# Nodes' places worked out in 128 rows behind the second table, and a written order with late sums in the message stage of a graph layer

## The chip, the core and the metric

The kernel runs on one core of a Trainium2 chip. The metric is the device time of one execution in microseconds (us). TensorE (PE), VectorE (DVE), ScalarE (ACT), GpSimd (POOL) and SyncE (SP) each run their own instructions in order, and wait for each other with semaphores. SP does no arithmetic here: it starts transfers between memory and the core's SBUF. POOL starts the indirect transfers, which gather rows of a table by a list of numbers.

## What is computed

One graph layer on 12,500 nodes with 96 features and 412,500 edges, all in float32. The edges are sorted by their target node `dst`.

```python
def _mlp(h, W, b, gamma, beta):
    h = relu(h @ W + b)
    mu, var = mean(h, axis=0), mean((h - mu)**2, axis=0)
    return gamma * (h - mu) * rsqrt(var + EPS) + beta

node_feat = _mlp(x, W_node, ...)
edge_feat = _mlp(edge_attr, W_edge, ...)          # 4 -> 96 features
message   = _mlp(concat([x[src], x[dst], edge_feat]), W_msg, ...)
agg       = segment_sum(message, dst)             # sum of the messages into each node
out       = layernorm(x + agg + node_feat)
```

## The kernel before

The product with `W_msg` is split into its three blocks of 96 rows. `x` times the first block gives the table `p_tab`, `x` times the second gives `q_tab`; both are stored in memory by `table()` (L137), which makes 14 columns of 128 nodes at a time, in 7 pieces, through the SBUF tile `trow`. A message then is relu(p_tab[src] + q_tab[dst] + edge part).

Edges go in tiles of 128, groups of 4 tiles (512 edges, 806 groups) and blocks of 4 groups (202 blocks). The stages, in the order of the program:

1. `p_tab` (L156), loads of small weights, and a check of the graph (L172 to L190).
2. Nodes' places (L192 to L201): for each edge, its target minus the first target of its group, as float32, written to memory as `rel_d`. The 413,696 numbers are laid out in 101 rows of 4096, and done in four parts of 1024 columns. Loads (`lin`, `first`) are issued by SP, the stores of `rel_d` by ACT. The tiles have two buffers each.
3. `fast()` (L286). Inside a block in which SP and POOL keep the written order (L309), it makes `q_tab`, then the node features (`nodes()`, L203, which end in 13 stores `y0_d`), then the mean and variance of the edge features (`edge_norm()`, L235: 26 loads of 8 blocks, for each block three matmuls on different rows of the array, one ReLU over all three on ACT, three `bn_stats` on DVE).
   While these run, POOL gathers ahead. `blocks()` (L298) gathers `p_tab` rows for the first 26 blocks (104 groups, 416 indirect transfers) into the tile `stage`, which has two buffers, and SP stores each block to `spill` in memory. Each `next(store)` puts one block's 16 gathers into POOL's order and its one store into SP's order at that point. So a store of `spill` stands in SP's queue between the stores and loads of the stage that is running, and the gathers of block b+2 can begin only when the store of block b has landed. After the 26 blocks, POOL fills a ring of 30 groups (L325).
4. The message stage (L327 to L439). The 176 late blocks take their `p_tab` rows from the ring, as POOL delivers them; the 26 early blocks take them back from `spill` (`fetch`, L410). The written order of blocks spreads the early ones among the late ones. For each block `load()` brings edge attributes, `rel_d` and four windows of `q_tab`, and `prepare()` makes the left operand `left` (relu of the edge part, and rows that mark the place: L371 matmuls into four PSUM banks, L373 on ACT, L374 on DVE). For each group `message()` makes z (4 matmuls, L380), adds the gathered rows (L386) and takes the ReLU (L387); `reduce()` multiplies the group's messages with themselves and with the marks of the targets (4 matmuls, L395) and adds the result to `agg` (L398) and to `gram` (L399), which gives mean and variance of the messages. `reduce` of a group stands one group behind its `message`. Here no order is fixed by hand: a scheduler orders each engine.
   POOL's part in it: after a group, the gather of the group 30 ahead is asked for (L436).
5. The final stage (L607): `agg` is scaled, turned to rows, added to `y0_d`, normalised and stored.

SBUF is handed out by pools: a pool that closes gives its space to the next, and the first write into the new tile waits until the last use of the old one is done. The tiles `lin` and `rlin` of stage 2 and `trow` of the second table lie in such shared space.

Of the kernel before, what the change touches and what calls it, by code (L numbers as in the profile page):

```python
# [11 lines left out]
F32 = mybir.dt.float32  # L12
I32 = mybir.dt.int32
# [9 lines left out]
P = 128  # L23
# [12 lines left out]
RW = 8 * GE  # L36
# [18 lines left out]
RING = 30  # L55
CL, CE = 2, 2
# [15 lines left out]
def gnn(ctx, tc, t):  # L72
# [7 lines left out]
    rel_d = dram.tile([1, EP], F32, name="rel_d")  # L80
# [56 lines left out]
    def table(out, w, work, ps, queues):  # L137

        rows = out.rearrange("(p b) f -> p b f", b=NB)
        for c in range(0, NB, CH):  # L140
            r = work.tile([P, CH, C], F32, name="trow", bufs=3)
            for j, i in enumerate(range(0, CH, NBK)):
                n = min(NBK, CH - i)
                pt = ps.tile([P, NBK, C], F32, name="pt", bufs=4)
                for g in range(n):
                    k = COL[c + i + g]
                    nc.tensor.matmul(pt[:, g, :], xp[:, k:k + P], w, start=True, stop=True)  # L147
                if j % 2:
                    nc.scalar.activation(r[:, i:i + n, :], pt[:, :n, :], AF.Copy)  # L149
                else:  # L150
                    nc.vector.tensor_copy(r[:, i:i + n, :], pt[:, :n, :])
            queues[c // CH % len(queues)].dma_start(rows[:, c:c + CH, :], r)
            yield

    with tc.tile_pool(name="win_w", bufs=1) as work, tc.tile_pool(name="win_ps", bufs=2, space=PSUM) as ps:
        for _ in table(p_tab, w_msg[:, 0, :], work, ps, (nc.sync, nc.scalar)):  # L156
            pass
# [34 lines left out]
    with tc.tile_pool(name="lin", bufs=2) as work:  # L192
        shape = "o (p g e) -> (o p) g e"
        for i in range(0, RW // GE, 2):
            lin = work.tile([EP // RW, 2, GE], I32, name="lin")
            nc.sync.dma_start(lin, t["dlin"].rearrange(shape, g=RW // GE, e=GE)[:, i:i + 2, :])
            first = work.tile([EP // RW, 2], I32, name="first")
            nc.sync.dma_start(first, t["base"].rearrange("o (p g) -> (o p) g", g=RW // GE)[:, i:i + 2])
            rlin = work.tile([EP // RW, 2, GE], F32, name="rlin")
            nc.vector.tensor_tensor(rlin, lin, first.unsqueeze(2).to_broadcast([EP // RW, 2, GE]), op=OP.subtract)  # L200
            nc.scalar.dma_start(rel_d.rearrange(shape, g=RW // GE, e=GE)[:, i:i + 2, :], rlin)  # L201
# [33 lines left out]
    def edge_norm():  # L235

        with tc.tile_pool(name="es", bufs=2) as work, tc.tile_pool(name="es1", bufs=1) as one, \
                tc.tile_pool(name="es_ps", bufs=2, space=PSUM) as ps:
            stats = one.tile([P, NS, NBL, 6], F32, name="estats")
            for b in range(NBL):  # L240
                if b % J == 0:
                    yield
                    ea = work.tile([P, J, GE], F32, name="ea")
                    n = min(J, NBL - b)
                    for i in range(NS):
                        nc.sync.dma_start(ea[Q * i:Q * i + 2 * EK, :n, :],
                                          t["ea"][EK * i:EK * (i + 2), b:b + n, :])
                pr = ps.tile([P, NS, GE], F32, name="pr")
                for i in range(NS):
                    nc.tensor.matmul(pr[:, i, :], wide[Q * i:Q * i + 2 * EK, :],  # L250
                                     ea[Q * i:Q * i + 2 * EK, b % J, :], start=True, stop=True)
                r = work.tile([P, NS, GE], F32, name="r")
                nc.scalar.activation(r, pr, AF.Relu)  # L253
                for i in range(NS):
                    nc.vector.bn_stats(stats[:, i, b, :], r[:, i, :])  # L255
# [30 lines left out]
    def fast(ring):  # L286
# [22 lines left out]
        with tc.manual_schedule(engines={ET.SP, ET.Pool}):  # L309
            with tc.tile_pool(name="tab_w", bufs=1) as work, tc.tile_pool(name="tab_ps", bufs=2, space=PSUM) as ps:  # L310
                for i, _ in enumerate(table(q_tab, w_msg[:, 1, :], work, ps, (nc.sync,))):
                    if i in (3, 6):
                        next(store)
            next(store)
            next(store)
            for i, _ in enumerate(nodes()):
                if i in (5, 12):
                    next(store)
            xpool.close()
            for i, _ in enumerate(edge_norm()):  # L320
                if i > 1 and i % 5:
                    next(store, None)
            for _ in store:
                pass
            got = {g: ahead_of(g) for g in range(SPILL, SPILL + RING)}  # L325

        with tc.tile_pool(name="fix", bufs=1) as fix, tc.tile_pool(name="msg", bufs=2) as work, \  # L327
# [3 lines left out]
            rhs = fix.tile([P, 2, BG, C], F32, name="rhs")  # L331
            nc.vector.tensor_copy(rhs[:C], w_e[:, None, None, :].to_broadcast([C, 2, BG, C]))
            for i in range(2):
                for k in range(BG):
                    nc.sync.dma_start(rhs[KR - 1:KR, i, k, :], bias)
# [3 lines left out]
            hb = [fix.tile([P, GT, P], F32, name=f"h{i}") for i in range(4)]  # L339
# [3 lines left out]
            eas = {}  # L343

            def load(s, b):

                n = min(BG, NG - b * BG)
                first = SPILL // BG
                c, o = ((b - first) // CL * CL + first, CL) if b >= first else (b // CE * CE, CE)
                if c not in eas:  # L350
# [8 lines left out]
                    base[:, b * BG:(b + 1) * BG], engines=[ET.DVE, ET.SP], min_val=0, max_val=N - 1,  # L359
                    skip_runtime_bounds_check_because="they are nodes' numbers")  # L360
                for i in range(n):
                    nc.sync.dma_start(rhs[C:C + WN, s % 2, i, :], q_tab[bass.ds(val[i], WN), :])
                return ea, val

            def prepare(s, b, ea):

                n = min(BG, NG - b * BG)
                x = left[s % 2]
                pr = ps.tile([C + WN, BG, GE], F32, name="pr", bufs=1)
                for i in range(n):  # L370
                    nc.tensor.matmul(pr[:, i, :], we[Q * i:Q * i + EK + 1, :],  # L371
                                     ea[Q * i:Q * i + EK + 1, :], start=True, stop=True)
                nc.scalar.activation(x[:C, :n, :], pr[:C, :n, :], AF.Relu)  # L373
                nc.vector.tensor_scalar(x[C:C + WN, :n, :], pr[C:, :n, :], 0.0, None, op0=OP.is_equal)  # L374

            def message(s, g, h, pg):
                n = min(GT, NT - g * GT)
                z = ps.tile([P, GT, C], F32, name="z")
                for i in range(n):
                    nc.tensor.matmul(z[:, i, :], left[s % 2][:KR, g % BG, i * P:(i + 1) * P],  # L380
                                     rhs[:KR, s % 2, g % BG, :], start=True, stop=True)
# [7 lines left out]
            def reduce(g, h, val):  # L389

                n = min(GT, NT - g * GT)
                pa = ps.tile([C + 1, P], F32, name="pa")
# [4 lines left out]
                to = agg[:, bass.ds(val, WN)]  # L397
# [4 lines left out]
            early, late = list(range(SPILL // BG)), list(range(SPILL // BG, NBL))  # L402
            order = []
            for i, b in enumerate(late):
                order.append(b)
                while early and (SPILL // BG - len(early)) * len(late) < i * (SPILL // BG):
                    order.append(early.pop(0))
            order += early

            def fetch(b):  # L410
                if b * BG < SPILL:
                    back = work.tile([P, BG, GT, C], F32, name="pb")
                    nc.sync.dma_start(back, spill[b].rearrange("p g (a c) -> p g a c", a=GT))
                    for i in range(BG):
                        got[b * BG + i] = back[:, i, :, :]

            ea, val = load(0, order[0])
            prepare(0, order[0], ea)
            fetch(order[0])
            last, n, ahead = None, 0, SPILL + RING  # L420
            for s, b in enumerate(order):
                more = s + 1 < len(order)
                if more:
                    ea, then = load(s + 1, order[s + 1])
                    fetch(order[s + 1])
                for g in range(b * BG, min((b + 1) * BG, NG)):
                    if g % BG == 1 and more:
                        prepare(s + 1, order[s + 1], ea)
                    h = hb[n % len(hb)]
                    n += 1  # L430
                    message(s, g, h, got.pop(g))
                    if last:
                        reduce(*last)
                    last = g, h, val[g % BG]
                    if g >= SPILL and ahead < NG:
                        got[ahead] = ahead_of(ahead)  # L436
                        ahead += 1
                val = then
            reduce(*last)  # L439
# [235 lines left out]
```

## Time and profile before

| what | value |
|---|---|
| median of 10 runs | 4306.22 us (4305.18 to 4308.59) |
| profiled execution: its own time, its span | 4305.96 us, 4304.2 us |
| PE busy | 3377.8 us (78%), 16,561 matmuls |
| DVE busy | 1812.4 us (42%) |
| ACT busy | 1132.6 us (26%) |
| POOL busy | 3054.0 us (71%), 3,231 instructions |
| moved by DMA | 271.03 MB, mean 63 GB/s |

The own time of the profiled execution is 1.76 us above its span and 0.26 us below the median. Busy times leave out register and branch instructions and the issuing of plain transfers; for POOL's gathers, the time on the engine is counted, and the gap to the next one is not. A matmul in float32 shows as two records. "PEclk" is the clock that TensorE was granted, as a share of the full one.

### The profile page before, as it was taken

To read this page: it belongs to the slowest core of one execution; us is meant where nothing else is said; L and a number is where in the kernel's file an instruction comes from. 1 tells how busy PE (TensorE), PEld (TensorE's weight loads), DVE (VectorE), ACT (ScalarE), POOL (GpSimd) and SP (SyncE) were. 2 spreads that over 40 slices of the span, in tenths; PEclk is the share of its full clock that TensorE was granted. 3 is DMA by queue.
4 is the path that set the end of the run, shared out by engine and by line. 5 is a ranking of instruction groups with operands and counts; after the bars stand their busy time and mean duration, and the time that the engine had idled before them with its cause. 6 is when DMAs were issued, how large, how long until landed. Compare 5 with 4: busy or idle time off the path is not lost. (4 is left out here: it accounts for less than half of the span.)

```text
span 4304.2 us, 52840 instructions
## 1 busy us (share of the span) xinstructions
PE 3377.8 (78%) x16561; PEld 2490.5 (58%) x16561; DVE 1812.4 (42%) x4227; ACT 1132.6 (26%) x1304; POOL 3054.0 (71%) x3231
## 2 busy tenths in 40 slices
PE   4089998778778887887787787777878888878787
PEld 4063222566666666666666666666666666656666
DVE  1057999533333333333333333333333333333334
ACT  0035776222122222222222222222222222212221
POOL 3067777777777777777777777777777777777772
PEclk9975555877777776778768777777776777777775
DMA  4045554222222222222222222222222222222223
GB/s 147 30 135 122 115 107 99 72 54 53 48 51 53 53 52 46 53 52 54 53 45 53 53 54 53 46 53 53 54 53 45 53 53 53 53 44 54 45 45 106
DMA packets 154490, 271.03 MB, mean 63 GB/s; under 512 B 83723, under 2 KB 84107, under 8 KB 153198
## 3 DMA queue, kind: packets, MB, share of 16 engines
q0 software_dynamic: 103136, 158.62, 17.8%
q1 hardware_dynamic: 47572, 96.59, 7.8%
q10 hardware_dynamic: 3496, 12.36, 0.9%
q8 instruction: 136, 2.23, 0.2%
q14 instruction: 150, 1.23, 0.1%
HBM read 225.97 MB, written 41.37 MB: 62 GB/s over the span
## 5 line engine op out<-in xcount | busy, mean ns | idle before, releaser
L290 POOL DMA_INDIRECT pg<-p_tab,src x2807 | 2655.1, 946 | 855.6 <-issue 765.9
L380 PEld LDWEIGHTS z<-rhs,left 128*128 128x128 f32 x6446 | 1111.6, 253 | 732.3 <-DVE hs L386 427.1
L395 PE MATMUL pa<-h 128*97 128x128 f32 x6446 | 1185.0, 343 | 365.7 <-ACT h L387 356.1
L380 PE MATMUL z<-rhs,left 128*128 128x96 f32 x6446 | 1240.5, 343 | 283.4 <-DVE hs L386 277.3
L395 PEld LDWEIGHTS pa<-h 128*97 128x97 f32 x6446 | 1011.4, 216 | 429.0 <-ACT h L387 419.7
L386 DVE TENSOR_TENSOR hs<-z,pg 128x384 f32<-128x384 f32 x702 | 391.0, 557 | 1935.9 <-DMA pg<-p_tab,src 1779.7
L387 ACT ACTIVATE h<-hs 128x384 f32<-128x384 f32 x806 | 420.9, 522 | 2581.6 <-DVE hs L386 1736.5
L290 POOL DMA_INDIRECT stage<-p_tab,src x416 | 398.0, 957 | 326.1 <-DMA spill<-stage 141.2
L371 PE MATMUL pr<-ea,we 6*127 6x512 f32 x1404 | 507.7, 870 | 40.0 <-DVE left L374 30.5
L374 DVE TENSOR_SCALAR left<-pr 31x2048 f32<-31x2048 f32 x202 | 462.9, 2291 | 19.2 <-ACT left L373 12.9
L373 ACT ACTIVATE left<-pr 96x2048 f32<-96x2048 f32 x202 | 375.0, 1857 | 111.8 <-PE pr L371 98.6
L250 PE MATMUL pr<-ea,wide 10*128 10x512 f32 x1212 | 396.1, 1096 | 9.3 <-DMA ea<-in_ea 9.3
L255 DVE BATCH_NORM_STATS2 estats<-r 128x6 f32<-128x512 f32 x606 | 369.5, 679 | 34.2 <-ACT r L253 30.3
L253 ACT ACTIVATE r<-pr 128x1536 f32<-128x1536 f32 x202 | 292.9, 1450 | 156.9 <-PE pr L250 156.9
L250 PEld LDWEIGHTS pr<-ea,wide 10*128 10x128 f32 x1212 | 113.2, 307 | 290.9 <-ACT r L253 267.1
L382 DVE TENSOR_TENSOR h<-rel,iota 128x124 f32<-128x124 f32 x806 | 207.6, 278 | 1.7 <-issue 0.4
L399 DVE TENSOR_TENSOR gram<-pa,gram 97x97 f32<-97x97 f32 x806 | 201.2, 250 | 6.6 <-DVE agg L398 6.5
L398 DVE TENSOR_TENSOR agg<-pa,agg 97x31 f32 x806 | 147.5, 183 | 130.5 <-PE pa L395 128.1
L147 PE MATMUL pt<-w_msg,xp 96*128 96x96 f32 x392 | 85.7, 423 | 138.9 <-ACT trow L149 131.4
L371 PEld LDWEIGHTS pr<-ea,we 6*127 6x127 f32 x1404 | 127.9, 237 | 104.4 <-DVE left L374 52.4
L147 PEld LDWEIGHTS pt<-w_msg,xp 96*128 96x128 f32 x392 | 84.1, 332 | 140.2 <-ACT trow L149 132.2
L386 DVE TENSOR_TENSOR hs<-z,pb 128x384 f32<-128x384 f32 x104 | 57.5, 553 | 84.6 <-ACT left L373 41.9
(97 smaller groups left out, 528.0 us busy)
## 6 DMA issues: line engine op xcount, KB each, us to landing
pg<-p_tab,src POOLq DMA_INDIRECT x2807
spill<-stage SPq DMA_DIRECT2D x26, 768.0 KB
pb<-spill SPq DMA_DIRECT2D x26, 768.0 KB
rhs<-q_tab SPq DMA_DIRECT2D x806, 11.6 KB
ea<-in_ea SPq DMA_DIRECT2D x75, 160.0 KB
ea<-in_ea SPq DMA_DIRECT2D x352, 20.0 KB
stage<-p_tab,src POOLq DMA_INDIRECT x416
q_tab<-trow SPq DMA_DIRECT2D x7, 672.0 KB
```

The lines of the kernel that those rows point to most:

```text
L250: nc.tensor.matmul(pr[:, i, :], wide[Q * i:Q * i + 2 * EK, :], ea[Q * i:Q * i + 2 * EK, b % J, :], start=True, stop=True)
L253: nc.scalar.activation(r, pr, AF.Relu)
L255: nc.vector.bn_stats(stats[:, i, b, :], r[:, i, :])
L290: nc.gpsimd.indirect_dma_start(out=pg[:, i, :], out_offset=None, in_=p_tab[:, :], in_offset=bass.IndirectOffsetOnAxis(ap=src[:, k:k + 1], ...
L371: nc.tensor.matmul(pr[:, i, :], we[Q * i:Q * i + EK + 1, :], ea[Q * i:Q * i + EK + 1, :], start=True, stop=True)
L373: nc.scalar.activation(x[:C, :n, :], pr[:C, :n, :], AF.Relu)
L374: nc.vector.tensor_scalar(x[C:C + WN, :n, :], pr[C:, :n, :], 0.0, None, op0=OP.is_equal)
L380: nc.tensor.matmul(z[:, i, :], left[s % 2][:KR, g % BG, i * P:(i + 1) * P], rhs[:KR, s % 2, g % BG, :], start=True, stop=True)
L382: nc.vector.tensor_tensor(h[:, :, C + 1:C + 1 + WN], rel[:, g, :].unsqueeze(2).to_broadcast([P, GT, WN]), iota[:, None, :].to_broadcast([P ...
L386: nc.vector.tensor_add(hs[:, :n, :], z[:, :n, :], pg[:, :n, :])
L387: nc.scalar.activation(h[:, :n, :C], hs[:, :n, :], AF.Relu)
L395: nc.tensor.matmul(pa[:, :C + 1 + WN], h[:r, i, :C + 1], h[:r, i, :C + 1 + WN], start=i == 0, stop=i == n - 1)
```

## The change

Four edits, and the loop that carries them.

- **Places.** The step moves out of stage 2 into a function `places()`, called behind the second table. The numbers are padded to 128 rows of 7 groups, done in parts of 2, 2, 2 and 1 groups. All transfers are on SP, and the store of a part is issued behind the load of the next.
- **Tables and stores.** The second table gets 8 PSUM buffers. The places of `next(store)` change: three within the second table, one behind `places()`, two within `nodes()` (behind the third and the ninth `y0_d` store), then one at 19 of the 26 loads of `edge_norm()` (73 in 100), the rest behind.
- **Edge statistics.** Matmuls are put in pairs into 4 PSUM tiles of two banks (before: three into 2 tiles of three), with one ReLU for each pair.
- **Message stage.** PE, DVE and ACT keep the written order too. z of group k+1 is asked for ahead of the additions of group k; the products of group k-1 follow; their sums are added at group k+4 (`SKEW = 5` behind k). Four groups' products share one PSUM tile. `prepare` is cut into two halves of two groups, at the third and fourth group of the block before. `left` is unchanged; the right operand `rhs` has 3 buffers (before 2), `h` has 6 (before 4), and `load` runs two blocks ahead (before one).

The core of the diff:

```diff
+    def places():
+        with tc.tile_pool(name="lin", bufs=2) as work, tc.tile_pool(name="lin1", bufs=1) as one:
+            first = one.tile([P, RW], I32, name="first")
+            nc.sync.dma_start(first, t["first"])
+            rows = rel_d.rearrange("o (p g e) -> (o p) g e", g=RW, e=GE)
+            parts = [slice(i, min(i + 2, RW)) for i in range(0, RW, 2)]
+            lins = []
+            for i in range(len(parts) + 1):
+                if i < len(parts):
+                    n = parts[i].stop - parts[i].start
+                    lins.append(work.tile([P, n, GE], I32, name="lin"))
+                    nc.sync.dma_start(lins[i], t["dlin"][:, parts[i], :])
+                    rlin = work.tile([P, n, GE], F32, name="rlin")
+                    nc.vector.tensor_tensor(rlin, lins[i], first[:, parts[i]]..., op=OP.subtract)
+                    lins[i] = rlin
+                if i:
+                    nc.sync.dma_start(rows[:, parts[i - 1], :], lins[i - 1])
...
-                    if i in (3, 6):
+                    if i in (1, 4, 6):
                         next(store)
-            next(store)
+            places()
             next(store)
             for i, _ in enumerate(nodes()):
-                if i in (5, 12):
+                if i in (2, 8):
                     next(store)
             xpool.close()
+            n = 0
             for i, _ in enumerate(edge_norm()):
-                if i > 1 and i % 5:
+                if 73 * i >= 100 * n:
                     next(store, None)
+                    n += 1
...
-                pr = ps.tile([P, NS, GE], F32, name="pr")
                 for i in range(NS):
-                    nc.tensor.matmul(pr[:, i, :], wide[...], ea[...], start=True, stop=True)
-                r = work.tile([P, NS, GE], F32, name="r")
-                nc.scalar.activation(r, pr, AF.Relu)
+                    k = NS * b + i
+                    if k % 2 == 0:
+                        pr = ps.tile([P, 2, GE], F32, name="pr")
+                    nc.tensor.matmul(pr[:, k % 2, :], wide[...], ea[...], start=True, stop=True)
+                    if k % 2:
+                        r = work.tile([P, 2, GE], F32, name="r", bufs=4)
+                        nc.scalar.activation(r, pr, AF.Relu)
...
+            with tc.manual_schedule(engines={ET.SP, ET.Pool, ET.PE, ET.DVE, ET.Activation}):
+                load(0)
+                fetch(0)
+                load(1)
+                edges(0)
+                prepare(0, 0)
+                prepare(0, BG // 2)
+                linear(0)
+                for k in range(n + SKEW):
+                    s, g = steps[min(k, n - 1)]
+                    if k < n and g % BG == 0:
+                        if s + 2 < len(order):
+                            load(s + 2)
+                        if s + 1 < len(order):
+                            fetch(s + 1)
+                    if k + 1 < n:
+                        linear(k + 1)
+                    if k < n:
+                        message(k)
+                    if 0 <= k - 1 < n:
+                        sums(k - 1)
+                    if k < n and s + 1 < len(order):
+                        if g % BG == 0:
+                            edges(s + 1)
+                        if g % BG >= BG // 2:
+                            prepare(s + 1, (g % BG - BG // 2) * (BG // 2))
+                    if k >= SKEW:
+                        add(k - SKEW)
+                    if k < n and g >= SPILL and ahead < NG:
+                        got[ahead] = ahead_of(ahead)
+                        ahead += 1
```

`linear` holds the z matmuls of L380, `message` L382 to L387, `sums` the matmuls of L395, `add` L398 and L399, `edges` the matmuls of L371, `prepare` L373 and L374. The numbers of matmuls, additions and gathers are those of before.

## The prediction

> **What bounds it now.** I read the groups of the page first, for an engine that never rests; then the waits, for who holds it up; then the timeline around the longest wait; then windows by stage.
>
> The groups (busy time, mean ns of one, idle before and its cause):
>
> ```profile
> L290 POOL DMA_INDIRECT pg<-p_tab,src x2807 | 2655.1, 946 | 855.6 <-issue 765.9
> L290 POOL DMA_INDIRECT stage<-p_tab,src x416 | 398.0, 957 | 326.1 <-DMA spill<-stage 141.2
> ```
>
> POOL's 71% hides a full engine: each gather takes 0.946 us and is followed by a gap of 0.30 us that no wait explains ("issue"). From 726.0 us (first `pg`) to 4236.3 us (end of the last) lie 2807 gathers: 3510.3 / 2807 = 1.2505 us each. The three longest whole windows hold 2402 in 3000 us, 1.249 each.
>
> The waits (total us, times, longest):
>
> ```profile
> DVE hs L386 <- DMA pg<-p_tab,src: 1779.7, 555, 4.7
> ACT trow L149 <- DMA rel_d<-rlin: 160.3, 1, 160.3
> POOL stage L290 <- DMA spill<-stage: 141.2, 3, 138.9
> ```
>
> In the message stage DVE waits for gathered rows 555 times: the consumers are quicker than POOL. So nothing done to PE, DVE or ACT there shortens the span; only POOL's own holes do, and there is one, of 138.9 us. The timeline shows its cause:
>
> ```profile
> 95.29 1.22 DVE L200 TENSOR_TENSOR rlin<-lin,first 101x1024 f32<-101x1024 int32 x1 [20.27 <-DMA first<-in_base]
> ...
> 127.86 1.23 DVE L200 TENSOR_TENSOR rlin<-lin,first 101x1024 f32<-101x1024 int32 x1 [31.34 <-DMA first<-in_base]
> ...
> 191.84 1.23 DVE L200 TENSOR_TENSOR rlin<-lin,first 101x1024 f32<-101x1024 int32 x1 [30.79 <-DMA first<-in_base]
> 211.38 1.02 DVE L151 COPY trow<-pt 128x384 f32<-128x384 f32 x2 [18.31 <-DMA rel_d<-rlin]
> ...
> 231.31 0.33 SPq L304 DMA_DIRECT2D spill<-stage  x1
> ...
> 236.29 0.94 POOL L290 DMA_INDIRECT stage<-p_tab,src  x1 [138.92 <-DMA spill<-stage]
> ```
>
> The four parts of the places come 32 us apart, on transfers of 101 rows. The second table's `trow` lies in their space and waits for the last store (211.4); the first `spill` store stands in SP's queue behind four table stores (231.3); it lands at 236.3, and only then may POOL fill the buffer a third time. Windows (busy us and count of PE, weights, DVE, ACT, POOL; clock; DMA share; GB/s):
>
> ```profile
> 97.40:236.30 138.90, 24.24 (x114) 24.24 (x114) 9.16 (x13) 3.66 (x9) 0.01 (x1) 1.00 0.12 46
> 726.00:4236.30 3510.30, 2791.76 (x14550) 2195.89 (x14545) 1334.19 (x3471) 792.23 (x1016) 2655.05 (x2807) 0.74 0.23 52
> ...
> 820.00:830.00 10.00, 9.83 (x77) 8.01 (x77) 6.83 (x19) 4.02 (x6) 7.56 (x9) 1.00 0.26 55
> ...
> 2030.00:2040.00 10.00, 9.00 (x38) 7.22 (x38) 2.57 (x11) 2.81 (x3) 7.57 (x9) 0.54 0.18 41
> ```
>
> The first is the hole, with every engine nearly idle. The last two are for the message stage below.
>
> **POOL's sum.** Before: start 55.1 (waits for `p_tab`); 416 x 1.249 = 519.6; waits for `spill` and `stage` 141.2 + 4.8 = 146.0; slow gathers and rest 5.3 (one of 3.41 us at 64.0 beside the 3.52 us subtraction L177, ten of 1.12 to 2.14 at 275 to 289); together 726.0. Then 3510.3, then 67.9 from the last gather to the end of the span: 4304.2. After: the gathers are as many, so 55.1 + 519.6 + 5.3 + S + 3510.3 + 67.9 + 0.3 = 4158.5 + S, with S the new waits for `stage` buffers. The 0.3 is the tail of the late sums: five additions of 0.18 + 0.25 us (L398, L399) are left, four of which run while ACT and PE finish the last group (0.44 + 1.6).
>
> **Places.** The 32 us per part go, since the table comes first. PE starts it at 74.9, as now, and makes 392 / 2 records at 0.215 us (168 in 36.2): 42 us, to 117; its eight PSUM buffers change nothing, as PE ran without a gap from 212.1 to 248.2. No row shows a 128-row transfer of 512 KB; the nearest is the `spill` store, 768 KB on 128 rows, 5.0 us from issue to landing (231.3 to 236.3). Bounds: 2 and 5; I take 3.5. The last table store lands at 122; then loads, 1.2 us subtractions and stores overlap two deep, and the last `rel_d` lands at 137 (132 to 147). What is late next: `bn_stats` of `nodes()` share that space, so DVE starts them at 137. PE and ACT do their part meanwhile.
>
> The Trainium skill (SBUF — State Buffer, "Who interferes with whom") speaks against this: a DVE operation with two SBUF inputs contends with GpSimd's reads. Three of four subtractions ran in POOL's hole; now all run beside gathers: 3 x 1.23 = 3.7 us by the rule. The one that had neighbours (95.29) left the gathers at 95.18 and 96.42 at 0.94: 0 us. The 3.4 us gather at 64.0 says the rule can hold. I take 0 and keep 4 for the range.
>
> **Stores in SP's queue (S).** POOL takes 20 us per block; block b+2 needs the store of b landed, 5 us after issue.
> - Stores 0 and 1 stand behind pieces 1 and 4 of the table (issue 87 and 106, land 92 and 111; needed 97 and 117). Store 2 lands at 124, needed 137; store 3, behind the places, at 142, needed 157. No wait: the hole is gone.
> - Store 4 stands behind the third `y0_d` store. From the trace: 25 `bn_stats` back to back at 0.61 (369.5 / 606) from 137 to 153; first update of x 1.7 later; `y0` 14.4 after that (274.8 to 289.2), 169; two copies, then the gap of 2.6 and the memset of `agg` of 10.5 (293.55) to 184; the third copy, its store, store 4 at 185, landed 190. Block 6 could start at 177.5. **S = 13.** If the places end 5 us earlier, 8; 10 later, 23.
> - Store 5 (behind the ninth, 19.3 us after the third by today's trace) lands at 209, needed 210: nothing, with 1 us to spare.
> - In `edge_norm` a store stands ahead of 19 loads. Load i goes out when iteration i-2 has left its buffer. Iterations now take 14.8 us when not held by a gather (loads at 362.77, 377.59, 392.41); 73 stores in 100 ask for 0.73 x 20 = 14.6. DVE sets the 14.8 (47.7 busy of 50), and its 606 `bn_stats` stay; pairs of 1024 in place of 1536 on ACT (1.45 us) fit below it. Start at 222, end at 222 + 25.25 x 14.8 = 596. The last store that POOL needs goes out at 222 + 22 iterations, so POOL leaves this stage at 247 + 22t against 580 + S: it costs only above t = 15.7 us. Zero; the range keeps t = 16.5 (S = 30).
>
> The ring of 30 groups is full at 593 + 150 = 743; the message stage starts some 45 us after the edge stage (740 to 784 now), at 641. That cover is 100 us; before it was 92.
>
> **Message stage.** Per group POOL leaves (4236.3 - 784.4) / 806 = 4.28 us. At full clock a block of 72 records takes 9.3 us (77 records in 10 us, window 820): 2.3 per group. Fixed order costs: DVE waits at the addition L386 for z and gathered rows; queued behind it are the marks of the next block and the sums of group k-5. The sums have had five groups' time and nobody reads `agg` in the stage; the marks are asked for one to two groups ahead of PE's z. PE's z(k+2) waits for the addition of k, as its two buffers force now too. SP loads two blocks ahead. The four targets that DVE reads into registers (L358) are read at the first addition instead, as often as before. Gain and loss: 0, since POOL ends last.
>
> A second rule of the Trainium skill against it (TensorE: Matmul & The Clock Gate, "HAM oscillation"): idle gaps over 3.4 us put the array at half clock. At half clock a group needs 2.0 (z) + 1.9 (products) + 1.0 (a quarter of the edge matmuls), 4.9 > 4.28. By the rule alone, a POOL that makes PE wait would make PE the bound. The rows say what happens: at 0.54 PE is busy 9.00 of 10 in 2030 to 2040 and as soon as work piles up, at 820, it has 1.00. So I take 0.
>
> Sum: 4158.5 + 13 = 4171.5 span, + 1.8 outside the span, + 0.3 to the median: **4173**.
>
> **Rivals.**
> - *No new wait* (S = 0 to 4): places land sooner, or POOL starts earlier. 4159 to 4164. For it: the queue is nearly empty then. Against: the memset alone is 10.5. 0.13.
> - *The edge stage becomes POOL's brake* (slower than before). The three matmuls of a block lie on different rows and overlap: 1.85 us for six records, where lone ones at 342.7 come every 0.86. If PSUM pairs let only two overlap, t = 14.8 x 1.5 = 22.2, S = 22t - 333 = 155: 4316. It beats the gain from t = 21.8. Against: four pairs hold eight matmuls. 0.05.
> - *The written order holds PE back*: at 4.4 us per group the stage would end at 641 + 806 x 4.4 = 4187, 4257 in all. For it: 9.00 of 10 busy at half clock is little room. 0.09.
> - *The hole stays* for some other shared space: 4306. Against: in the order of the changed program, the table's first copies wait for nothing of the places. 0.03.
>
> The forecast has 0.70. A measurement here can tell about 0.2% (9 us). Faster: 0.70 + 0.13 + 0.08 = 0.91; same 0.03; slower 0.06. Range: from S = 0 with a start 4 us sooner (4156) to S = 30 with 4 us for the port and a few tenths of a per cent of the third rival: 4205.
>
> **What would show it.** POOL: no wait for `spill` over 25 us; the last gather ends near 4103. DVE's waits for `pg` stay near 1780 us. `rel_d` landed by 140. A wait of 8 to 23 us of `stage` near 178 us. It is wrong if POOL waits for `pg` buffers, if waits for `spill` come back in the edge stage, or if the waits of L386 move from `pg` to z.

## Result and profile after

The changed kernel takes 4214.96 us in the median of 8 runs (4210.85 to 4217.02); the kernel before took 4307.17 us beside it (28 runs). The ratio is 0.9785, with a 95% interval of 0.9776 to 0.9793: 92 us less. The forecast was 4173, with a range up to 4205. So the direction and the main gain came as told, and some 40 us of it were lost again. The profiled execution has a span of 4208.9 us; the forecast for the span was 4171.5.

The groups of the page, POOL's gathers (busy, mean ns of one, idle before):

```profile
L304 POOL DMA_INDIRECT pg<-p_tab,src x2807 | 2677.3, 954 | 855.6 <-issue 732.5
L304 POOL DMA_INDIRECT stage<-p_tab,src x416 | 399.5, 960 | 207.2 <-issue 120.2
```

The idle time ahead of the `stage` gathers fell from 326.1 to 207.2: the hole is gone. But one `pg` gather now takes 954 ns in place of 946 in the mean. Over 2807 gathers that is 22 us, and nothing in the forecast moved it.

The waits (total us, times, longest):

```profile
DVE hs L431 <- DMA pg<-p_tab,src: 1450.8, 540, 7.1
DVE left L413 <- ACT left L412: 640.9, 403, 14.8
DVE hs L431 <- PE z L420: 37.8, 31, 3.2
POOL stage L304 <- DMA stage<-p_tab,src: 24.3, 22, 3.1
POOL stage L304 <- DMA spill<-stage: 8.9, 2, 8.6
```

POOL's wait for `spill` went from 141.2 to 8.9 us. A wait that was 4.8 us before is 24.3 now: gathers into `stage` that wait for the landing of a gather eight places earlier. DVE still waits for gathered rows 540 times and hardly for PE, so POOL ends last as before. Its total for these rows fell from 1779.7 to 1450.8 us, though, where the forecast had it near 1780: in the written order DVE now also waits for ACT's half of `left` (640.9 us; before, one wait of 12.9). That costs nothing as long as POOL ends last.

The timeline of the first stages:

```profile
127.26 2.39 DVE L208 TENSOR_TENSOR rlin<-lin,first 128x1024 f32<-128x1024 int32 x2 [10.85 <-DMA lin<-in_dlin]
128.51 1.97 POOL L304 DMA_INDIRECT stage<-p_tab,src  x1 [0.30 <-issue]
...
139.04 14.61 DVE L223 BATCH_NORM_STATS2 nstats<-agg 96x6 f32<-96x512 f32 x25 [2.36 <-DMA rel_d<-rlin]
...
186.11 0.32 SPq L318 DMA_DIRECT2D spill<-stage  x1
...
190.49 0.94 POOL L304 DMA_INDIRECT stage<-p_tab,src  x1 [8.58 <-DMA spill<-stage]
```

The last `rel_d` landed at 139 (forecast 137), store 4 went out at 186.1 (185), and POOL went on at 190.5 (190). The first `pg` gather came at 608.6 (593), the end of the last at 4141.2 (4103).

**The sum, measured.** The waits above hold the 0.30 us gap that follows every gather anyway, and that the forecast counts within its 1.249 us per gather; without it, the waits for `spill` are 8.3 us and those for landings 17.6. Against the forecast, from the gathers' records: waits for `spill` 8.3 in place of 13 (-4.7); waits for landings 17.6, for which the forecast has no term (+17.6); slow gathers and rest 7.7 in place of 5.3 (+2.4); the start +0.3; the `pg` stretch 3532.6 in place of 3510.3 (+22.3); the tail -0.4. 4171.5 + 37.5 = 4209.0, with 4208.9 measured. Two terms of about 20 us each are to be explained.

**Theory.** (A) In the message stage, the marks (L427: `rel` compared with `iota`, both in SBUF) now start together with gathers and stretch them. (B) In the edge stage, a `spill` store and the edge loads behind it in SP's queue go out back to back, and gathers that fly at that time land late. **Rivals.** To A: the gathers are stretched by something that the first stages set, or by the late sums. To B: the store alone, or the loads alone, do it.

### The profile page after: what moved, and what is told of

The parts are those of the page before. It is cut to its first block, busy times and chain, and to the rows that moved or that the text cites. A ratio compares the mean times of both kernels' runs of the same rounds, so it can differ in the third digit from the quotient of the medians.

```text
span 4208.9 us, 52605 instructions
## 1 busy us (share of the span) xinstructions
PE 2823.0 (67%) x16561; PEld 2361.4 (56%) x16561; DVE 1851.1 (44%) x4430; ACT 1139.6 (27%) x1606; POOL 3077.7 (73%) x3231
## 3 DMA queue, kind: packets, MB, share of 16 engines
q14 instruction: 152, 1.25, 0.1%
## 5 line engine op out<-in xcount | busy, mean ns | idle before, releaser
L420 PE MATMUL z<-rhs,left 128*128 128x96 f32 x6446 | 1147.6, 336 | 1232.2 <-issue 841.7
L420 PEld LDWEIGHTS z<-rhs,left 128*128 128x128 f32 x6446 | 1039.4, 245 | 1475.7 <-issue 912.5
L444 PE MATMUL pa<-h 128*97 128x128 f32 x6446 | 1084.1, 324 | 4.3 <-ACT h L432 4.3
L431 DVE TENSOR_TENSOR hs<-z,pg 128x384 f32<-128x384 f32 x702 | 389.9, 555 | 1469.6 <-DMA pg<-p_tab,src 1450.8
L444 PEld LDWEIGHTS pa<-h 128*97 128x97 f32 x6446 | 964.8, 207 | 4.9 <-ACT h L432 4.9
L413 DVE TENSOR_SCALAR left<-pr 31x1024 f32<-31x1024 f32 x403 | 495.7, 1230 | 640.9 <-ACT left L412 640.9
L304 POOL DMA_INDIRECT stage<-p_tab,src x416 | 399.5, 960 | 207.2 <-issue 120.2
L412 ACT ACTIVATE left<-pr 96x1024 f32<-96x1024 f32 x403 | 403.5, 1001 | 17.4 <-PE pr L404 16.1
L267 ACT ACTIVATE r<-pr 128x1024 f32<-128x1024 f32 x303 | 293.4, 1024 | 141.0 <-PE pr L263 118.7
L263 PEld LDWEIGHTS pr<-ea,wide 10*128 10x128 f32 x1212 | 202.1, 318 | 187.0 <-issue 96.0
L427 DVE TENSOR_TENSOR h<-rel,iota 128x124 f32<-128x124 f32 x806 | 222.8, 276 | 0.2
L404 PE MATMUL pr<-ea,we 6*127 6x512 f32 x1404 | 202.5, 645 | 24.0 <-DMA ea<-rel_d 12.4
L404 PEld LDWEIGHTS pr<-ea,we 6*127 6x127 f32 x1404 | 55.1, 183 | 53.5 <-DVE left L413 23.4
## 6 DMA issues: line engine op xcount, KB each, us to landing
rhs<-q_tab SPq DMA_DIRECT2D x806, 11.6 KB
```

Source lines behind the costliest of these rows:

```text
L263: nc.tensor.matmul(pr[:, k % 2, :], wide[Q * i:Q * i + 2 * EK, :], ea[Q * i:Q * i + 2 * EK, b % J, :], start=True, stop=True)
L304: nc.gpsimd.indirect_dma_start(out=pg[:, i, :], out_offset=None, in_=p_tab[:, :], in_offset=bass.IndirectOffsetOnAxis(ap=src[:, k:k + 1], ...
L404: nc.tensor.matmul(prs[s][:, i, :], we[Q * i:Q * i + EK + 1, :], block[s][Q * i:Q * i + EK + 1, :], start=True, stop=True)
L412: nc.scalar.activation(x[:C, part, :], pr[:C, part, :], AF.Relu)
L413: nc.vector.tensor_scalar(x[C:C + WN, part, :], pr[C:, part, :], 0.0, None, op0=OP.is_equal)
L420: nc.tensor.matmul(zs[k][:, i, :], left[s % 2][:KR, g % BG, i * P:(i + 1) * P], rhs[:KR, s % RB, g % BG, :], start=True, stop=True)
```

## Experiments

"Before" in these runs is the kernel before on the same chip (4302 to 4304 us); 0.001 of the ratio is 4.3 us.

**Each half alone.** `e1_places_only` joins the first stages of after with the message stage of before, `e2_message_only` the other way round:

```diff
 # e1: after up to and with this line
 got = {g: ahead_of(g) for g in range(SPILL, SPILL + RING)}
-# message stage of after: linear, message, sums, add in a written order
+# message stage of before: message, reduce, order left to the scheduler
```

> The stages up to the ring as in after, the message stage as in before (no written order there). Theory: the gain comes from POOL's hole alone, and the written order costs 22 us, as its marks (two inputs in SBUF) start together with gathers and stretch them. So the first pg gather stays at 609, its gathers take 946 ns in the mean in place of 954, and the time is 4215 - 22 = 4193 us. Rival: the order is neutral and the gathers are stretched by something that the earlier stages set (the ring's lead, the phase of transfers): 954 ns stay, 4215. Second rival: the order helps, and without it POOL finds its ring buffers taken: over 4220.

> The stages up to the ring as in before, with the hole; the message stage as in after. Theory: 4307 + 22 = 4329 us, the marks lie on the gathers' heads, pg gathers of 954 ns. Rival (the order costs nothing by itself): 4307 and 946 ns. If the order hid a gain that POOL's bound kept back, DVE would wait for pg as long as before and the time would still be 4307.

Measured: places only 4187.48 us, 0.9732 (0.9719 to 0.9745); message stage only 4320.40 us, 1.0043 (1.0029 to 1.0057). The line of the `pg` gathers, first of the one:

```profile
L304 POOL DMA_INDIRECT pg<-p_tab,src x2807 | 2654.1, 946 | 855.5 <-issue 700.7
```

and of the other:

```profile
L292 POOL DMA_INDIRECT pg<-p_tab,src x2807 | 2670.6, 951 | 855.6 <-issue 656.3
```

The first stages alone gain 2.7%, more than the whole change. The written order is a loss of 18 us with the hole, and of about 23 without it (0.9785 against 0.9732). It stretches the gathers and brings nothing that POOL's bound would let through. The first rival to A falls, but for 3 ns: with before's first stages the mean is 951, with after's 954.

**The marks moved, left out, and made in another way.** `e3_marks_ahead` moves them by one place in DVE's order:

```diff
 # at step k
 message(k)
+marks(k + 1)
 sums(k - 1)
 add(k - SKEW)
 # and in message(k):
-nc.vector.tensor_tensor(h[:, :, C + 1:C + 1 + WN], rel..., iota..., op=OP.is_equal)
```

> After, with one move: the marks of group k+1 stand behind the addition of the gathered rows of group k and ahead of the two late sums, so they start some 0.45 us after that addition starts, in place of 0.9. Theory (the marks cost only when they lie on the head of a gather): pg gathers near 946 ns, 4215 - 22 = 4193 us. Rival (the order as such, or the late sums themselves, stretch the gathers; these two also read SBUF): 954 ns stay, 4215. A miss of another kind: the marks find another gather's head there, over 4215.

`e8_no_marks` drops that line altogether:

> After, with the marks of the message stage left out (the columns hold zeros from the start, so the sums per node are left out of what is computed). Theory: no DVE operation with two SBUF inputs is left in the message stage's loop, so the gathers fall to their floor of 0.942 us: 0.012 x 2807 = 34 us less than after, 4181. Rival (the stretch comes from the additions or from memory traffic): 954 ns stay and 4215.

`e11_one_input_marks` leaves it at its place, with one tensor input:

```diff
-nc.vector.tensor_tensor(h[:, :, C + 1:C + 1 + WN], rel..., iota..., op=OP.is_equal)
+for i in range(GT):
+    nc.vector.tensor_scalar(h[:, i, C + 1:C + 1 + WN], iota, rel[:, g, i:i + 1], None, op0=OP.is_equal)
```

> After, with the marks at their place, but made by four operations with one tensor input each (iota, against one number per row) in place of one with two tensor inputs. Theory (only a DVE operation with two SBUF inputs holds up a gather): pg gathers fall to 944 to 946 ns, 4185 to 4193 us. Rival (any DVE operation between SBUF and SBUF does, and four of them last longer): 954 ns or more, 4210 to 4230.

Measured: marks ahead 4185.26 us, 0.9727 (0.9714 to 0.9740); no marks 4184.09 us, 0.9720 (0.9702 to 0.9737); one input 4186.43 us, 0.9725 (0.9712 to 0.9739). All three show 944 ns per `pg` gather. Their pages, in this order:

```profile
L304 POOL DMA_INDIRECT pg<-p_tab,src x2807 | 2650.6, 944 | 855.5 <-issue 656.5
L304 POOL DMA_INDIRECT pg<-p_tab,src x2807 | 2648.7, 944 | 855.5 <-issue 659.8
L304 POOL DMA_INDIRECT pg<-p_tab,src x2807 | 2650.9, 944 | 855.5 <-issue 728.4
```

and, in the groups of DVE, the marks of the third:

```profile
L428 DVE TENSOR_SCALAR h<-iota,rel 128x31 f32<-128x31 f32 x3224 | 572.3, 251 | 0.1
```

The four operations cost DVE 572 us in place of 223, run at the same place beside the gathers, and hardly stretch any: 67 of 2807 lie above 0.96 us, the longest at 0.99 (after: 222, up to 1.20). So it is not DVE's time beside the gathers, but the operation with two tensor inputs from SBUF. The kind and the shape of the operation changed together with the number of inputs; the operations in the first stages, below, show the same hold with other kinds and shapes. The late sums stay in all three, and the gathers are at their floor; the second rival to A falls. "No marks", which leaves out a part of the sums, was expected at 4181 and came 3 us higher: its mean gather is 943.6 ns, not 942, and its first `pg` gather came at 611.2.

How one operation of 0.28 us does it is seen in the timeline of after, at a group where the gathered rows were there early:

```profile
1520.34 0.19 DVE L456 TENSOR_TENSOR agg<-pa,agg 97x31 f32 x1
1520.45 0.25 DVE L457 TENSOR_TENSOR gram<-pa,gram 97x97 f32<-97x97 f32 x1
1520.60 1.11 POOL L304 DMA_INDIRECT pg<-p_tab,src  x1 [0.30 <-DVE agg L456]
1520.62 0.28 DVE L427 TENSOR_TENSOR h<-rel,iota 128x124 f32<-128x124 f32 x1
...
1523.28 0.94 POOL L304 DMA_INDIRECT pg<-p_tab,src  x1 [0.30 <-issue]
```

The marks start 0.02 us after the gather, and the gather takes 1.11 us; one with no marks at its head takes 0.94. The same place with the marks ahead:

```profile
1524.18 0.56 DVE L434 TENSOR_TENSOR hs<-z,pg 128x384 f32<-128x384 f32 x1 [4.00 <-DMA pg<-p_tab,src]
1524.66 0.28 DVE L425 TENSOR_TENSOR h<-rel,iota 128x124 f32<-128x124 f32 x1
...
1525.27 0.94 POOL L304 DMA_INDIRECT pg<-p_tab,src  x1 [0.30 <-DMA pg<-p_tab,src]
```

DVE's addition begins when the last gather of its group lands. A landing comes 2.5 us after its gather's start (median in the stage), two periods of 1.25, so it falls near the start of another gather. Marks that follow the addition at 0.48 us lie in the middle of that gather. In after they come behind two more additions and reach the next head. All 806 marks of a trace, by their start against a gather's start (number of marks, how many of them have a gather over 0.96 us, the gathers' mean in us):

| marks start | before | after | marks ahead |
|---|---|---|---|
| 0.2 to 0.1 us earlier | 80, 19, 0.961 | 64, 18, 0.954 | 23, 9, 0.959 |
| 0.1 to 0 us earlier | 32, 29, 1.058 | 123, 123, 1.047 | 27, 18, 1.003 |
| 0 to 0.1 us later | 20, 11, 1.056 | 72, 72, 1.133 | 44, 1, 0.947 |
| 0.1 to 0.2 us later | 22, 8, 1.034 | 28, 7, 1.008 | 43, 0, 0.943 |
| 0.2 to 0.8 us later | 463, 2, 0.945 | 291, 0, 0.944 | 580, 0, 0.943 |

Marks that start further off are left out. Of the 222 long gathers of after, 220 have marks that start within 0.2 us of their own start. In after, marks that start 0.05 us earlier cost 0.10 us and those 0.05 later 0.19: later start, later end, longer wait. With marks from 0.1 us earlier to 0.12 us later every gather is long, beyond 0.12 none. That is what an exclusive hold would do which lasts to the operation's end, and which the gather meets once, 0.12 to 0.13 us after its start. The first stages fit the same working. Ten updates of `x` (two SBUF inputs, 1.50 us each) run back to back in after, and ten gathers beside them are long, at 1.12 to 1.20 us:

```profile
156.90 12.95 DVE L229 SCALAR_TENSOR_TENSOR xp<-agg,norm_node,xp 96x1250 f32<-96x1250 f32 x9
159.53 1.12 POOL L304 DMA_INDIRECT stage<-p_tab,src  x1 [0.30 <-issue]
160.95 1.13 POOL L304 DMA_INDIRECT stage<-p_tab,src  x1 [0.30 <-issue]
```

For these ten, for three subtractions of the places and for the subtraction L179, a meeting 0.118 to 0.132 us after the gather's start and a wait to the end of DVE's operation give the gather's length, from 1.12 to 4.03 us.

The Trainium skill (SBUF — State Buffer, "Who interferes with whom") states such a hold for a DVE operation with two SBUF inputs, against a GpSimd instruction that reads SBUF; each gather has its list of rows, `src`, in SBUF. The page also takes it, as an inference by its own words, that such an operation does not hold up the writing of descriptors. These rows do not speak against that: marks that start 0.2 to 0.8 us into a gather cost nothing (none of 291). That it is the reading of `src` that is held is argued, not shown.

Not explained: with the marks ahead, those 0 to 0.1 us after a gather's start cost nothing (1 of 44). They follow the addition L434 there and `gram` in after; the recorded start may stand differently to the reading itself. This is only argued.

**The edge stage.** `e4_split_store` cuts a store in four, `e9_no_edge_loads` drops the loads:

```diff
 # e4, in blocks()
     gather(b * BG + i, pg[:, i, :, :])
-nc.sync.dma_start(spill[b], pg.rearrange("p g a c -> p g (a c)"))
+    nc.sync.dma_start(spill[b][:, i, :], pg[:, i, :, :].rearrange("p a c -> p (a c)"))
 # e9, in edge_norm()
-for i in range(NS):
+for i in range(NS if b < 2 * J else 0):
     nc.sync.dma_start(ea[...], t["ea"][...])
```

> After, with each spill store cut into its four groups (192 KB each, issued as soon as the group's four gathers have landed) in place of 768 KB at once. Theory: in the edge stage the store and the three loads behind it go out together, gathers then land 10 us late in place of 4, and POOL waits at the gather eight later. With the store spread, POOL's waits for stage's landing fall from 24.3 us to under 10, the first pg gather comes near 595, 4215 - 15 = 4200 us. Rival (the edge loads alone hold the gathers up): waits stay near 24 and the time at 4215. Second rival: more stores in SP's queue hold up the edge loads, over 4215.

> After, with 24 of the 26 loads of edge attributes in the edge stage left out (the statistics use the first two loads' data again). Theory of the burst (768 KB store and 480 KB of loads back to back): with one of the two gone, POOL's waits for stage's landing fall from 24.3 to under 10 us, about 4200 to 4205. Rival (the store alone delays the landings): waits stay near 24 and 4215. SP then is never held by edge buffers, so stores leave as soon as their gathers have landed.

Measured: 4194.52 us, 0.9749 (0.9736 to 0.9762), and 4191.62 us, 0.9740 (0.9722 to 0.9757). The wait, with the store in pieces:

```profile
POOL stage L304 <- DMA stage<-p_tab,src: 8.6, 4, 2.9
```

and without the loads:

```profile
POOL stage L307 <- DMA stage<-p_tab,src: 7.1, 3, 3.8
```

SP's timeline in after, for the stretch that these waits lie in:

```profile
360.94 0.35 SPq L318 DMA_DIRECT2D spill<-stage  x1
361.46 2.03 SPq L257 DMA_DIRECT2D ea<-in_ea  x3
380.79 0.35 SPq L318 DMA_DIRECT2D spill<-stage  x1
381.30 6.56 SPq L257 DMA_DIRECT2D ea<-in_ea  x6
```

The loads stood in the queue behind a store that waited for its gathers; so the first load follows the store by 0.5 us. From a gather's issue to its landing it then takes 5.5 us in the median and 10.4 in the upper tenth (300 to 400 us of the trace); in pieces 4.1 and 7.9, without loads 2.4 and 3.0. In before's edge stage, where most loads left 4 us or more behind a store, it is 3.9 and 7.6 (350 to 450 us); two of its waits for landings, at 638.0 and 698.5, come some 11 us after a store with a load right behind it (626.36 and 626.87, 686.81 and 687.41). Each gather waits for the landing of the eighth one before it, 8 x 1.25 = 10 us, so only landings later than 10 us stop POOL. The first `pg` gather comes at 599.0 and 597.3, in place of 608.6. The loads alone do not do it (they are all there in pieces), nor does the store alone (it is whole without loads): B holds, and both its rivals fall. The two edits win back 10 and 11 us, not all 17.6: a few waits for landings stay, and the waits for `spill` are 11.6 and 9.8 us. The other 6 to 7.5 us of the two gains come from elsewhere: their `pg` gathers take 951 and 952 ns.

**The places: layout or position.** `e6_101_rows` keeps the new position with the old layout, `e7_places_first` the new layout with the old position:

```diff
 # e6
-RW = 7                                    # 128 rows of 7 groups
+RW = 8                                    # 101 rows of 8 groups
 # e7
 with tc.manual_schedule(engines={ET.SP, ET.Pool}):
+    places()
     ...                                   # second table
-    places()
```

> After, with the places in 101 rows of eight groups (before's layout) at their new place behind the second table; all else as in after. Theory: the 101 rows cost about 30 us per part[...], so the last rel_d lands near 137 + 85 = 220; bn_stats of the nodes and the spill stores in the queue wait, POOL's wait is about 80 to 100 us: 4295 to 4315. So the layout makes the gain, not the place. Rival (the order on the queues did it): the transfers overlap now, the rel_d lands by 160 and the time stays within 20 us of 4215.

> After, with the places (128 rows) put ahead of the second table, where they were in before in the order of the program. Theory: the places take 15 to 20 us in 128 rows, the second table's tiles wait for them, as its memory is shared; table and nodes come some 15 us later, and POOL's wait for the first stores grows by about that much: 4215 + 10 to 20. Rival (the place is what counts): near 4310.

Measured: 101 rows 4318.25 us, 1.0037 (1.0024 to 1.0050); places first 4198.11 us, 0.9754 (0.9737 to 0.9772). The timeline with 101 rows:

```profile
140.29 1.23 DVE L208 TENSOR_TENSOR rlin<-lin,first 101x1024 f32<-101x1024 int32 x1 [25.06 <-DMA lin<-in_dlin]
157.79 1.22 DVE L208 TENSOR_TENSOR rlin<-lin,first 101x1024 f32<-101x1024 int32 x1 [16.27 <-DMA lin<-in_dlin]
189.19 1.22 DVE L208 TENSOR_TENSOR rlin<-lin,first 101x1024 f32<-101x1024 int32 x1 [30.18 <-DMA lin<-in_dlin]
220.62 1.22 DVE L208 TENSOR_TENSOR rlin<-lin,first 101x1024 f32<-101x1024 int32 x1 [30.21 <-DMA lin<-in_dlin]
252.01 14.62 DVE L223 BATCH_NORM_STATS2 nstats<-agg 96x6 f32<-96x512 f32 x25 [30.16 <-DMA rel_d<-rlin]
254.47 0.94 POOL L304 DMA_INDIRECT stage<-p_tab,src  x1 [98.41 <-DMA spill<-stage]
```

From the second on, the parts are 31 us apart again, behind the table as they were ahead of it, and the hole is back at another place (98.4 us, and a wait of 28.4 from 275). With 128 rows ahead of the table, the places run from 74.5 to 91.8 us:

```profile
79.27 1.23 DVE L208 TENSOR_TENSOR rlin<-lin,first 128x1024 f32<-128x1024 int32 x1 [4.80 <-DMA lin<-in_dlin]
79.64 1.67 POOL L304 DMA_INDIRECT stage<-p_tab,src  x1 [0.30 <-issue]
80.85 1.22 DVE L208 TENSOR_TENSOR rlin<-lin,first 128x1024 f32<-128x1024 int32 x1 [0.36 <-DMA lin<-in_dlin]
81.61 1.28 POOL L304 DMA_INDIRECT stage<-p_tab,src  x1 [0.30 <-issue]
```

So without the layout the rest of the first stages' edits gains nothing: 1.0037, against 1.0043 for the written order alone. With the layout, the move is not needed. What the layout would bring by itself, in the kernel before, is untested: the new places of the stores, the eight PSUM buffers and the pairs of the edge statistics came along in both of these runs. My expectation for the 128 rows in front (10 to 20 us worse) was wrong: `bn_stats` of the nodes then start at 126.7 in place of 139.0, since their memory is free once the last table store has landed, and the waits for `spill` fall to 6.8 us. That brings the first `pg` gather to 604.5, 4 us earlier; the other 7 us of the profile's gain lie in the `pg` stretch (951 ns per gather). The subtractions beside gathers show the same hold as the marks, here 0.73 and 0.34 us.

**Both mends, and after once more.** `e5_marks_and_store` has the edits of marks ahead and of the split store; `e10_all_three` also the places first; `e12_after_again` is after unaltered.

> The marks ahead of the late sums and the spill store in four pieces, together. Theory (two separate costs, both on POOL's path): they add up. First pg gather at 599 as with the pieces alone, pg gathers 1.249 us apart as with the marks ahead alone, 69 us behind the last: 599 + 3505 + 69 = 4173 us span, about 4173 to 4176 in time. Rival (they share a cause, or DVE or PE ends last before that): no better than the marks ahead alone, 4185.

> The same two, and the places ahead of the second table. Theory (places ahead of the table cost nothing and bring the nodes forward by some 10 us, so the wait for spill near 180 us shrinks from 10 to 4.5 and 2): first pg gather at 593 to 596, 4167 to 4171. Rival (the gain of the places' other position was the chance phase of the marks, which is gone here): as with the two alone, 4173 to 4176.

> The changed kernel once more, unaltered, beside the others. If its 954 ns per pg gather (five other kernels with the same order showed 951 to 952) is a property of the kernel, it comes back, at a ratio of 0.9785; if it is the chance of one execution, 951 ns and about 0.977.

Measured: 4177.60 us, 0.9704 (0.9691 to 0.9717); 4170.20 us, 0.9691 (0.9678 to 0.9704); after again 4214.78 us, 0.9791 (0.9778 to 0.9804). The two costs add up, and without them the time is within 5 us of the forecast: in the records of the two edits, the first `pg` gather at 599.1, 3506.3 us to the last one's start, 68.9 behind it, 4174.2 in all. The version with all three edits is the fastest, 1.0% below after by the ratios (0.9691 / 0.9791 = 0.9898). Whether the third edit adds anything stays open: its interval touches that of the two, and its profiled execution, the slowest of its five (4177.45), shows the first `pg` gather at 601.3, not at 593 to 596. After again has 954.4 ns per `pg` gather. So the 951 to 952 ns of the five other kernels with this order, one trace each, look like a matter of their different first stages and not of chance; how these would set the phase of marks and gathers is open. It is worth 6 to 8 us.

## Why the prediction was right and wrong

- **The bound and the hole: right.** POOL ended last, the hole of 138.9 us went, and no large wait took its place. The edge stage and the order of PE did not become the bound: DVE waited 37.8 us for z, and none of the rivals' ends came.
- **"The 32 us per part go, since the table comes first": right size, wrong reason.** They went with the 128 rows. The two changes came together, and the sum gave the credit to the move without asking what each would do alone; that the size came out right was luck of the bundle.
- **Places and S: sizes near.** `rel_d` landed at 139 for 137, the waits for `spill` were 8.9 for 13. The memset and the second table ran as told.
- **"Zero" for the edge stage: failed, 17.6 us.** The step followed when stores and loads go out, and asked whether POOL would wait for a store. It did not ask what a store and loads that go out together do to the gathers in flight. Before's row "4.8 us, 5 times" showed that wait. The sum of before has it (146.0 = 141.2 + 4.8); the sum of after drops it without a reason, since S was worked out from stores alone.
- **"Message stage: gain and loss: 0, since POOL ends last": failed, 22.3 us.** The step looked for what could make POOL wait and took a gather's own duration as fixed. An engine that is ahead can still make the bound engine's instructions longer. The same kind of operation as the subtractions runs 806 times in the message stage beside POOL's gathers, and the new order moved just that one. As an estimate, a full hold by each (0.28 us in the trace), 806 x 0.28 = 226 us, would have been the far end of its cost; before's own records (58 gathers over 0.96 us) gave the near end, about 6.5.
- **The port rule at 0: set from a near miss.** It had been weighed for four subtractions only, and one of them was read as "0 us". That subtraction started 0.12 us after one gather's start, and ended 0.03 us before the next gather would have met it: it fell between the two meetings by chance. Three of the four stretched a gather in after (128.51, 134.52 and 136.10 us, +1.8 us together). The ten gathers of 1.12 to 2.14 us in before, which the sum put down as slow, lie beside the ten updates of `x` and show the hold too.
- **The range** added up gains and losses of the steps that were on the list. Two terms of about 20 us were not on it. (The last line of the sum adds up to 4173.6, not 4173.)

## What to carry over

When one engine bounds a stage, ask of every edit what it does to that engine's own instructions, and not only to its waits: operations with two inputs in SBUF that move against GpSimd's gathers can change each gather's length. When an edit changes a layout and a position together, cost each alone. And of transfers put into one queue, ask which of them the queue will release at the same moment, and what else is in flight then.

## What the runs showed of the hardware

- An operation of 0.28 us with two SBUF inputs, started within 0.1 us of a gather's start, stretches it by 0.10 to 0.19 us in the mean; one of 1.2 us by up to 1.03 (the gather at 128.51). The gather meets it once, 0.12 to 0.13 us after its start, and waits for its end. Four operations with one tensor input leave the mean at 944 ns.
- Transfers of 101 rows of 4 KB pieces came 31 to 33 us apart per part at either place; those of 128 rows were done in 17 us for all four parts.
- A store of 768 KB and three loads of 160 KB sent back to back go with 5.5 us from a gather's issue to its landing in the median and 10.4 in the upper tenth; with the store alone it is 2.4 and 3.0.
- With the written order PE's busy time in the `pg` stretch is 2251 us in place of 2792, for nearly as many records (14,503 and 14,550), at a granted clock of 0.76 and 0.74. The cause stays open. None of it shows in the time, since POOL ends last.
